# Moving two more units of a product to GpSimd, and shifting the offsets of GpSimd's operands, in a four-layer state-space kernel

## The chip, the core and the metric

The kernel runs on one core of one Trainium2 chip, in float32. The metric is the device time of one execution, in microseconds; before the change the median of three runs is 19150.31 us (19148.47 to 19160.53).

## What is computed

Eight images of 48 x 48 pixels and 96 channels pass through four layers, each with a group norm ahead of it and a residual sum behind it. Layers 0 and 3 (`ss2d`) and layer 2 (`lines`) are selective scans over the pixels in four directions, with 192 inner channels and 16 states; layer 1 (`spectral`) is a filtered two-layer network. The core of a scan layer is, for each direction:

```
def step(h, inp):
    u, dl, Bv, Cv = inp
    dA = jnp.exp(dl[..., None] * A)
    h = h * dA + (dl * u)[..., None] * Bv[:, :, None, :]
    y = jnp.einsum('bkdn,bkn->bkd', h, Cv)
    return (h, y)
...
delta = jax.nn.softplus(dts + dt_projs_bias)
_, ys = jax.lax.scan(step, h0, (u_t, d_t, B_t, C_t))
ys = jnp.moveaxis(ys, 0, -1) + xs * Ds
```

Here u is a convolved and Silu-gated input, dl (delta) a step size for each channel and pixel, and B and C are 16 numbers for each pixel. In ss2d one scan runs over all 2304 pixels of an image; in lines each of the 48 rows or columns starts from zero again.

## The kernel before

**Tiling.** A direction of an image is cut into five blocks of columns, four of 480 pixels and one of 384 (BLKS). With 8 images and 4 directions a scan layer has 160 blocks, and the three scan layers 480. The 192 channels x 16 states of a block are 24 *units* of 128 partitions (32 channels x 4 states) by n pixels. Three units make a *slot* (ORDER: channel half and group of four states), two slots a *turn*, four turns a block. Slots 0 and 1 belong to turn 0, up to 6 and 7 in turn 3.

**What a turn does.** All of it is in `scans`. A room (tile `dbu`, six units of m columns) is filled, scanned and multiplied in place:
- `make_dbu` (line 257) multiplies du by B. Even slots do their three units on VectorE. Odd slots are split by ON_POOL: so many of the last units on GpSimd, the others on VectorE. VectorE reads B from a copy in PSUM (`ps_b`, one bank), which `copy_b` (line 238) makes on ScalarE, seven times a block; GpSimd reads it from SBUF (`bc`).
- `make_da` (line 281) makes exp(dl x A) on ScalarE into `ps_da`, two units to a pair and two such tiles.
- `scan` (line 289) runs the recurrence on VectorE over a pair of units, three times a turn.
- `make_hc` (line 295) multiplies three units by C in place on GpSimd, twice a turn.
- `reduce` (lines 315 and 317) sums over states on TensorE.

**Order.** There is no scheduler: the program order in the turn loop is each engine's order. On VectorE a turn is: scan of pair 0, product of the next turn's even slot, scan of pair 1, product of the next turn's odd slot, scan of pair 2. So slots 2 and 3 are filled in turn 0, slots 4 and 5 in turn 1, 6 and 7 in turn 2, and the next block's 0 and 1 in turn 3. On GpSimd it is: product with C of the last turn's odd slot, product with B for the next turn's odd slot, product with C of this turn's even slot. `aside`, called twice a turn, puts in between: loads, one step of a neighbour image's convolution or norm (`side`), and a step of `stage1`, which prepares the block after the next. In ss2d, stage1's softplus (line 648, with a table load before it and one behind it) falls into turn 3 and du = dl x u (line 439, GpSimd) into the ends of turn 3 and turn 0. In lines, a Silu (line 808) falls into turn 1, one (line 766) into turn 3, a softplus (line 794) and du into turn 0. Also in lines, the gated result is projected (line 831, TensorE) and added to x (lines 837 and 839, VectorE) in turn 1.

**Layout.** Blocks of lines have m = n columns. In ss2d a unit has m = n + 2: a column that comes from the block before and one that goes to the next, one at each end, with the pixels between them (`at` starts at 1); blocks alternate in direction, so that a room's last column is the next block's first. delta and du lie side by side in `dds` (line 427 stores them to DRAM, line 212 loads them back repeated over partitions as `dd`). A `bc` tile holds one zero, then n values of B, then n of C, so that B with its leading zero starts at 0 and C at 1 + n.

The GpSimd products that the change shifts besides these are du (line 439) and the gate of the output (line 563, y times z).

Of the kernel before, what the change touches and what calls it, by code (L numbers as in the profile page):

```python
# [9 lines left out]
F32 = mybir.dt.float32  # L10
# [7 lines left out]
DH = 96  # L18
# [4 lines left out]
P = 128  # L23
SEG = 48
BLKS = [(0, 10), (10, 10), (20, 10), (30, 10), (40, 8)]
BMAX = 480
WMAX = BMAX + 2
NG = 8
ORDER = [(0, sg) for sg in range(4)] + [(1, sg) for sg in range(3, -1, -1)]
LOAD_BC = (2, 3, 6, 7)  # L30
# [1 line left out]
NBUF = 6  # L32
# [4 lines left out]
NM = 3  # L37
FAR = 1e30
CH = 96
ON_POOL = {1: 1, 3: 2, 5: 2, 7: 2}  # L40


DIRS_SS = [(False, False), (True, False), (False, True), (True, True)]
# [15 lines left out]
class Block:  # L59
# [9 lines left out]
    def columns(self, restart):  # L69

        self.mirrored = not restart and self.blk % 2 == 1
        self.back = self.rev != self.mirrored
        if restart:
            self.m = self.n
            self.at = self.by = slice(0, self.n)
            return
        self.m = self.n + 2
        self.at = slice(1, self.n + 1)
        self.came, self.goes = (self.m - 1, 0) if self.back else (0, self.m - 1)

        self.by = slice(0, self.n + 1) if self.back else slice(1, self.n + 2)

# [11 lines left out]
def vss_stack_kernel(ctx: ExitStack, tc: tile.TileContext, i: dict, out: bass.AP):  # L94
    nc = tc.nc
# [88 lines left out]
    def scans(dirs, order, restart, a, pools, ps, stage1, opening, done, side, tail):  # L184
# [6 lines left out]

        blocks = [Block(job, k, blk, n == 0, n == len(BLKS) - 1, dirs[k][1])
                  for job in range(nb) for k in order
                  for n, blk in enumerate(range(len(BLKS))[::-1 if dirs[k][1] else 1])]
# [2 lines left out]
        turns = [(b, q) for b in blocks for q in range(NG // 2)]  # L199
        nt = len(turns)  # L200
        rooms = [pools["dbu"].tile([P, 6 * WMAX], F32, tag="dbu", name="dbu") for _ in range(NG // 2)]
        bufs = [pools["bc"].tile([P, 1 + 2 * BMAX], F32, tag=f"bc{n}", name=f"bc{n}") for n in range(NBUF)]
        for buf in bufs:
            nc.gpsimd.memset(buf[:, 0:1], 0.0)
        dbus, das, bps, bcs, ys = {}, {}, {}, {}, {}
        later, ends = {}, []
        free = {n: 0 for n in range(NBUF)}
# [7 lines left out]
        def load_bc(t):  # L215

            b, slot = blocks[t // NG], t % NG
            sg = ORDER[slot][1]
            other = t - slot + NG - 1 - slot
            n = min(free, key=lambda n: free[n])  # L220
            free[n] = other
            r = bufs[n]
            rows4 = b.bcd[8 * sg:8 * sg + 8, :].rearrange("(s w) n -> s (w n)", w=2)
            nc.sync.dma_start(r[:, 1:1 + 2 * b.n], rows4.unsqueeze(0).to_broadcast([32, 4, 2 * b.n]))

            lead = b.at.start
            bcs[t] = bcs[other] = r[:, 1 - lead:1 - lead + b.m], r[:, 1 + b.n:1 + 2 * b.n]

        def copy_b(t):

            if t >= NG * len(blocks):
                return
            b, slot = blocks[t // NG], t % NG
            if slot == NG // 2:
                bps[t] = bps[t - 1]
                return
            bps[t] = ps("b", 1)
            nc.scalar.copy(bps[t][:, :b.m], bcs[t][0])  # L238

        def units(tile, b, lo, hi):  # L240
            return tile[:, lo * b.m:hi * b.m].rearrange("p (u m) -> p u m", m=b.m)
# [182 lines left out]
        b.bcd = pools["dr"].tile([2 * NS, b.n], F32, tag=f"bcd_{b.n}", name="bcd")  # L424

    def store_dd(b, half):
        nc.sync.dma_start(b.dd[half].rearrange("j (g m) -> g j m", g=3), b.dds[:, half, :2 * b.m])

    def sizes(b, half):

        t = b.dds[:, half]
        return [t[:, n * b.m:(n + 1) * b.m][:, b.at] for n in range(2)]

    def make_du(b, half, u):


        n = b.n
        dt, du = sizes(b, half)
        nc.gpsimd.tensor_mul(rows(du, n), rows(dt, n), u)  # L439
        if b.m == b.n:  # L440
            at = SEG - 1 if b.rev else 0
            nc.gpsimd.memset(rows(dt, n)[:, :, at:at + 1], FAR)
        elif half == 0:
            ends = b.dds[:, :, :2 * b.m].rearrange("p h (t m) -> p h t m", t=2)
            nc.gpsimd.memset(ends[:, :, :, b.came:b.came + 1], FAR)
            nc.gpsimd.memset(ends[:, :, :, b.goes:b.goes + 1], 0.0)


    def ss2d(l, xin, xout, b0=0):
        stack = ExitStack()  # L450
        pools, ps = scan_pools(stack)
# [3 lines left out]
        wt, big, zp, lnp, xio = pool("wt", 1), pool("big", 3), pool("z", 1), pool("ln", 2), pool("xio", 2)  # L455
# [21 lines left out]
        us, yss, zs = {}, {}, {}  # L477
# [38 lines left out]
        def post(b, blks=BLKS):  # L516

            y = yss[b]
            var = small.tile([CH, L // CH], F32, tag="var", name="var")
            v0, v1 = min(r0 for r0, nr in blks) * W // CH, max(r0 + nr for r0, nr in blks) * W // CH  # L520
            for r0, nr in blks:
                n = nr * SEG
                s = slice(r0 * W, r0 * W + n)
                pm = side_psum()
                for half in range(2):
                    nc.tensor.matmul(pm[:DH, :n], lhsT=mean, rhs=y[:, half, s], start=(half == 0), stop=(half == 1))
                yield
                yc = y[:, :, s]
                nc.vector.tensor_sub(yc, yc, pm[:DH, :n].unsqueeze(1).to_broadcast([DH, 2, n]))
                yield  # L530
                sq = lnp.tile([DH, 2, BMAX], F32, tag="sq", name="sq", bufs=1)
                nc.scalar.activation(sq[:, :, :n], yc, AF.Square)
                yield
                pv = side_psum()
                for c in range(n // CH):
                    for half in range(2):
                        nc.tensor.matmul(pv[:CH, c:c + 1], lhsT=sq[:, half, c * CH:(c + 1) * CH], rhs=ones,
                                         start=(half == 0), stop=(half == 1))
                yield
                nc.vector.tensor_copy(var[:, r0 * W // CH:(r0 * W + n) // CH], pv[:CH, :n // CH])  # L540
                yield
            nc.scalar.activation(var[:, v0:v1], var[:, v0:v1], AF.Sqrt, bias=eps5[:CH])
            yield
            nc.vector.reciprocal(var[:, v0:v1], var[:, v0:v1])
            yield
            for r0, nr in blks:
                n = nr * SEG
                s = slice(r0 * W, r0 * W + n)
                z = lnp.tile([DH, 2, BMAX], F32, tag="zin", name="zin", bufs=1)
                nc.sync.dma_start(z[:, :, :n], zs[b][:, :, s])  # L550
                xi = xio.tile([C, BMAX], F32, tag="xi", name="xi")
                nc.sync.dma_start(xi[:, :n], xin[b][:, s])
                pr = side_psum()
                for c in range(n // CH):
                    at = r0 * W // CH + c
                    nc.tensor.matmul(pr[:DH, c * CH:(c + 1) * CH], lhsT=var[:, at:at + 1].to_broadcast([CH, DH]),
                                     rhs=wc["ident"], start=True, stop=True)
                yield
                for half in range(2):
                    nc.vector.scalar_tensor_tensor(y[:, half, s], y[:, half, s], w[f"{l}_nw"][:, half:half + 1], pr[:DH, :n],  # L560
                                                   ALU.mult, ALU.mult)
                yield
                nc.gpsimd.tensor_mul(y[:, :, s], y[:, :, s], z[:, :, :n])
                po = side_psum()
                for half in range(2):
                    nc.tensor.matmul(po[:C, :n], lhsT=wnb[:, half, :], rhs=z[:, half, :n], start=(half == 0), stop=False)
                yield
                for half in range(2):
                    nc.tensor.matmul(po[:C, :n], lhsT=w[f"{l}_out"][:, half, :], rhs=y[:, half, s],
                                     start=False, stop=(half == 1))  # L570
                yield
                nc.vector.tensor_add(xi[:, :n], xi[:, :n], po[:C, :n])
                yield
                nc.sync.dma_start(xout[b][:, s], xi[:, :n])
# [38 lines left out]
        def stage1(b):  # L613
            n = b.n
            u = b.view(us[b.job], dirs[b.k][0])
# [23 lines left out]
                raw(0)  # L639

            def s4():
                b.dds = pools["dds"].tile([DH, 2, 2 * WMAX], F32, tag="dds", name="dds")
                biased(0)
                raw(1)

            def s6():
                both = b.dds[:, :, b.at]
                nc.scalar.activation(both, both, AF.Softplus)  # L648

            def du(half):  # L650
# [35 lines left out]
    def lines(xin, xout):  # L686
        stack = ExitStack()
        pools, ps = scan_pools(stack)
# [15 lines left out]
        for name in ("l2_outpt", "l2_out", "l2_inu"):  # L704
            shape = i[name].shape
            t = pools["dbu"].tile([P, 6 * WMAX], F32, tag="dbu", name="dbu")
            t = t[:shape[0], :int(np.prod(shape[1:]))]
# [35 lines left out]
        def stage1(b):  # L743
            n = b.n
# [44 lines left out]

            def s6():  # L790
                nc.sync.dma_start(b.bcd, b.bcl[:2 * NS, :n])
                b.dds = pools["dds"].tile([DH, 2, 2 * WMAX], F32, tag="dds", name="dds")
                for half in range(2):
                    nc.scalar.activation(sizes(b, half)[0], got[half][:DH, :n], AF.Softplus,  # L794
                                         bias=w["l2_dtb"][:, b.k, half:half + 1])
# [353 lines left out]
```

## Time and profile before

The profile is one execution: 19152.15 us, of which the span from the first to the last instruction is 19150.3 us.

| Stage | us from the start |
|---|---|
| ss2d, layer 0 (first scan 119, last 5827) | 119 to 5827 |
| spectral, layer 1 | 5827 to 7260 |
| lines, layer 2 | 7260 to 13276 |
| opening of layer 3 | 13276 to 13404 |
| ss2d, layer 3 | 13404 to 19118 |

| Group | count | busy us | mean ns |
|---|---|---|---|
| VectorE scan, line 289 | 5760 | 11863.3 | 2072 |
| GpSimd product with C, line 295 | 3840 | 10685.9 | 2796 |
| ScalarE exponential, line 281 | 11520 | 7428.3 | 648 |
| VectorE product with B, line 257 | 3840 | 4414.3 | 1150 |
| GpSimd product with B, line 257 | 1920 | 3101.7 | 1615 |
| ScalarE copy of B, line 238 | 3360 | 1805.0 | 537 |
| GpSimd du, line 439 | 640 | 815.1 | 1274 |

Means mix shapes: 480 and 384 columns, one to three units. A line of the timeline gives the start in us, the duration in us, the engine, the source line, the operation, what it writes and reads, and in brackets how long its engine was idle before it and what ended that. Instructions of one engine overlap a little in the records (a scan of 2.16 us is followed by the next instruction 2.07 us after its start), so a duration is not quite what an engine loses by an instruction; from start to start is. A line of the waits gives the total, how many times, and the longest.

### The profile page before, as it was taken

What the parts mean: (1) busy time and instruction counts of PE and PEld (TensorE: products, weight loads), DVE (VectorE), ACT (ScalarE), POOL (GpSimd) and SP (SyncE); (2) the same over time, 40 slices, a digit from 0 to 9 for tenths busy, and PEclk for the clock granted to TensorE, in tenths of its full rate; (3) what the DMA queues carried; (4) which work ended last, traced back from release to release, by engine and by line L of the source; (5) the groups of instructions that cost most, each with busy time, mean ns of one, the idle gap of its engine ahead of it and who ended that gap; (6) DMA issues with size and microseconds to landing.
All of it is one profiled execution on the core that took longest, in us unless ns stands there. A gap on an engine that the chain in (4) does not pass through costs nothing.

```text
span 19150.3 us, 170303 instructions
## 1 busy us (share of the span) xinstructions
PE 15031.5 (78%) x53500; PEld 4344.3 (23%) x53500; DVE 16643.8 (87%) x11289; ACT 14070.7 (73%) x20982; POOL 15110.6 (79%) x8304
## 2 busy tenths in 40 slices
PE   6777777777777997888888888887677777777776
PEld 1211211211214562222222222222121121121121
DVE  7999999999993227999999999997999999999998
ACT  6777877877872227888888888886778778778776
POOL 6899999899891006777777777776898998999998
PEclk7776776776767777887888888888777677677676
DMA  4444444444443324444444444443444444444444
GB/s 136 166 160 162 165 162 165 164 164 163 159 169 61 48 44 141 152 145 150 149 146 151 143 152 149 144 150 123 161 165 158 165 165 158 165 165 161 163 163 143
DMA packets 768469, 2831.72 MB, mean 148 GB/s; under 512 B 235724, under 2 KB 298668, under 8 KB 640926
## 3 DMA queue, kind: packets, MB, share of 16 engines
q1 hardware_dynamic: 767558, 2820.84, 44.7%
q8 instruction: 418, 6.85, 0.2%
q14 instruction: 493, 4.04, 0.1%
HBM read 2373.39 MB, written 447.18 MB: 147 GB/s over the span
## 4 chain that ended last, share of the span: by engine, by line
DVE 26%; PE 22%; ACT 18%; issue 16%; POOL 13%; DMA 4%; SPq 0%; DVEq 0%; POOLq 0%; ACTq 0%
DVE dbu L289 15%; POOL dbu L295 10%; DVE dbu L257 10%; PE ps_s L759 5%; ACT ps_da L281 5%; ACT L281 4%; PE ps_y L315 3%; PE ps_h L989 2%; POOL dbu L257 2%; PE ps_side L501 2%; PE ps_y L1002 2%; PE ps_s L831 1%; PE ps_s L630 1%; DMA dd<-dd 1%; DMA dd<-dds 1%
## 5 line engine op out<-in xcount | busy, mean ns | idle before, releaser
L289 DVE TENSOR_TENSOR_SCAN dbu<-ps_da,dbu 128x964 f32<-128x964 f32 (+3 forms) x5760 | 11863.3, 2072 | 884.6 <-ACT ps_da L281 862.4
L295 POOL TENSOR_TENSOR dbu<-dbu,bc 128x1440 f32<-128x1440 f32 (+1 forms) x3840 | 10685.9, 2796 | 2290.8 <-DVE dbu L289 2202.6
L281 ACT ACTIVATE ps_da<-dd,w_l_a 128x482 f32<-128x482 f32 (+3 forms) x11520 | 7428.3, 648 | 2851.4 <-DVE dbu L289 2636.8
L315 PE MATMUL ps_y<-dbu,w_red 128*32 128x480 f32 (+1 forms) x23040 | 4910.5, 745 | 2690.4 <-POOL dbu L295 2684.9
L317 PE MATMUL ps_y<-dbu,w_red 128*32 128x480 f32 (+1 forms) x7680 | 4869.1, 745 | 0.0
L257 DVE TENSOR_TENSOR dbu<-dd,ps_b 128x1443 f32<-128x1443 f32 (+10 forms) x3840 | 4414.3, 1150 | 264.6 <-ACT ps_b L238 217.0
L257 POOL TENSOR_TENSOR dbu<-dd,bc 128x962 f32<-128x962 f32 (+6 forms) x1920 | 3101.7, 1615 | 79.6 <-DMA dd<-dd 39.7
L315 PEld LDWEIGHTS ps_y<-dbu,w_red 128*32 128x32 f32 x23040 | 757.2, 126 | 6562.2 <-POOL dbu L295 4864.9
L238 ACT COPY ps_b<-bc 128x482 f32<-128x482 f32 (+3 forms) x3360 | 1805.0, 537 | 319.2 <-DVE dbu L257 288.5
L759 PE MATMUL ps_s<-xpad,w_l_cw 128*128 128x480 f32 (+1 forms) x2560 | 1758.4, 840 | 2.3 <-ACT xpad L142 1.6
L501 PE MATMUL ps_side<-xpad,w_l_cw 128*128 128x480 f32 (+1 forms) x2880 | 1604.8, 685 | 4.5 <-ACT xpad L142 4.5
L281 ACT ACT_TABLE_LOAD x986 | 1265.0, 1283 | 17.6
L131 POOL MEMSET w_l_cw<- 128x1760 f32 (+1 forms) x3 | 5.8, 1941 | 1340.3 <-DVE x L969 1334.9
L439 POOL TENSOR_TENSOR dds<-dds,u 96x480 f32<-96x480 f32 (+1 forms) x640 | 815.1, 1274 | 199.7 <-ACT dds L648 199.7
L630 PE MATMUL ps_s<-u,w_l_xp 96*38 96x480 f32 (+1 forms) x1280 | 932.7, 869 | 2.8 <-ACT dds L624 1.5
L620 PE MATMUL ps_s<-bcl,dtw 6*96 6x480 f32 (+1 forms) x1280 | 837.9, 742 | 108.1 <-ACT dds L624 99.8
L311 PE MATMUL ps_y<-ysum,w_ident 96*96 96x480 f32 (+1 forms) x960 | 753.2, 875 | 118.2 <-ACT ysum L671 118.1
L501 PEld LDWEIGHTS ps_side<-xpad,w_l_cw 128*128 128x128 f32 x2880 | 567.5, 222 | 1119.5 <-issue 907.5
L759 PEld LDWEIGHTS ps_s<-xpad,w_l_cw 128*128 128x128 f32 x2560 | 524.0, 210 | 1085.0 <-issue 999.6
L317 PEld LDWEIGHTS ps_y<-dbu,w_red 128*32 128x32 f32 x7680 | 697.3, 126 | 0.0
L776 PE MATMUL ps_s<-ub,w_l_xp 96*38 96x480 f32 (+1 forms) x640 | 382.7, 734 | 245.8 <-ACT ub L766 245.8
L800 PE MATMUL ps_s<-xpad,w_l_inz 96*96 96x480 f32 (+1 forms) x640 | 494.0, 904 | 97.6 <-ACT dds L794 80.9
(146 smaller groups left out, 11996.1 us busy)
## 6 DMA issues: line engine op xcount, KB each, us to landing
dd<-dd SPq DMA_DIRECT2D x512, 1446.0 KB
bc<-bcd SPq DMA_DIRECT2D x1536, 480.0 KB
dd<-dd SPq DMA_DIRECT2D x256, 1440.0 KB
dd<-dds SPq DMA_DIRECT2D x512, 361.5 KB
dd<-dd SPq DMA_DIRECT2D x128, 1158.0 KB
bc<-bcd SPq DMA_DIRECT2D x384, 384.0 KB
dd<-dds SPq DMA_DIRECT2D x256, 360.0 KB
dd<-dd SPq DMA_DIRECT2D x64, 1152.0 KB
```

The lines of the kernel that those rows point to most:

```text
L238: nc.scalar.copy(bps[t][:, :b.m], bcs[t][0])
L257: engine.tensor_mul(o, du, by.unsqueeze(1).to_broadcast([P, hi - lo, by.shape[1]]))
L281: nc.scalar.activation(da[:, at:at + b.m], b.got[half][:, u % 3, 0, :], AF.Exp, scale=a[:, b.k, ci:ci + 1])
L289: nc.vector.tensor_tensor_scan(db, da, db, 0.0, ALU.mult, ALU.add)
L295: nc.gpsimd.tensor_mul(h, h, bcs.pop(2 * t + sub)[1].unsqueeze(1).to_broadcast([P, 3, n]))
L315: nc.tensor.matmul(y[32 * g:32 * g + 32, :n], lhsT=wc["red"][:, :32], rhs=hc[:, g, b.at], start=False, stop=(slot == 3))
L317: nc.tensor.matmul(y[DH:, :n], lhsT=wc["red"][:, 32:], rhs=hc[:, 2, b.at], start=(slot == 0), stop=(slot == 3))
L439: nc.gpsimd.tensor_mul(rows(du, n), rows(dt, n), u)
L501: nc.tensor.matmul(pu[:, :n], lhsT=flat[:, at:at + P], rhs=xpad[:, r0 + dy:r0 + dy + nr, dx:dx + W], start=(tap == 0), stop=(tap == 8))
L620: nc.tensor.matmul(got["p"][:DH, :n], lhsT=dtw[2 * NS:, b.k, half, :], rhs=b.bcl[2 * NS:, :n], start=True, stop=True)
L630: nc.tensor.matmul(got["p"][:NBC, :n], lhsT=w[f"{l}_xp"][:, b.k, half, :], rhs=u[:, half], start=(half == 0), stop=(half == 1))
L759: nc.tensor.matmul(got["u", half][:, :n], lhsT=flat[:, at:at + P], rhs=shifted(off), start=(tap == 0), stop=(tap == 3))
```

## The change

- ON_POOL goes from {1: 1, 3: 2, 5: 2, 7: 2} to {1: 2, 3: 2, 5: 3, 7: 2}: nine units of 24 on GpSimd in place of seven. Slot 5 has none left on VectorE, and its copy of B to PSUM is left out. In the built program VectorE has 480 products fewer, ScalarE 480 copies fewer, GpSimd as many products as before, of which 960 are one unit larger.
- In ss2d a unit is n + 4 columns wide in place of n + 2 (the pixels start at 1 as before; the two added columns lie at the end). A scan covers 2m columns, so 968 for 964.
- A `bc` tile begins with two zeros (LEAD) in place of one. `dds` begins two elements into its tile, and so does z of the output's gate.
- The rooms are set to zero once a layer; the columns that carry FAR and zero in `dds` are written as runs of three and one.

```diff
-WMAX = BMAX + 2
+WMAX = BMAX + 4
+LEAD = 2
...
-ON_POOL = {1: 1, 3: 2, 5: 2, 7: 2}
+ON_POOL = {1: 2, 3: 2, 5: 3, 7: 2}
...
-        self.m = self.n + 2
+        self.m = self.n + 4
         self.at = slice(1, self.n + 1)
-        self.came, self.goes = (self.m - 1, 0) if self.back else (0, self.m - 1)
+        self.came, self.goes = (self.n + 1, 0) if self.back else (0, self.n + 1)
...
-        bufs = [pools["bc"].tile([P, 1 + 2 * BMAX], F32, tag=f"bc{n}", name=f"bc{n}") for n in range(NBUF)]
+        bufs = [pools["bc"].tile([P, LEAD + 2 * BMAX], F32, tag=f"bc{n}", name=f"bc{n}") for n in range(NBUF)]
         for buf in bufs:
-            nc.gpsimd.memset(buf[:, 0:1], 0.0)
+            nc.gpsimd.memset(buf[:, :LEAD], 0.0)
+        for room in rooms:
+            nc.gpsimd.memset(room, 0.0)
...
-            nc.sync.dma_start(r[:, 1:1 + 2 * b.n], rows4.unsqueeze(0).to_broadcast([32, 4, 2 * b.n]))
-
-            lead = b.at.start
-            bcs[t] = bcs[other] = r[:, 1 - lead:1 - lead + b.m], r[:, 1 + b.n:1 + 2 * b.n]
+            nc.sync.dma_start(r[:, LEAD:LEAD + 2 * b.n], rows4.unsqueeze(0).to_broadcast([32, 4, 2 * b.n]))
+
+            lo, hi = LEAD - b.at.start, LEAD + b.n
+            bcs[t] = bcs[other] = r[:, lo:hi + b.at.start], r[:, hi:hi + b.n]
...
+            if ON_POOL.get(slot) == 3:
+                return
             bps[t] = ps("b", 1)
-            nc.scalar.copy(bps[t][:, :b.m], bcs[t][0])
+            nc.scalar.copy(bps[t][:, :bcs[t][0].shape[1]], bcs[t][0])
...
+    def make_room(b, pools):
+        b.room = pools["dds"].tile([DH, LEAD + 4 * WMAX], F32, tag="dds", name="dds")
+        b.dds = b.room[:, LEAD:LEAD + 4 * b.m].rearrange("p (h t m) -> p h t m", h=2, t=2)
...
-            ends = b.dds[:, :, :2 * b.m].rearrange("p h (t m) -> p h t m", t=2)
-            nc.gpsimd.memset(ends[:, :, :, b.came:b.came + 1], FAR)
-            nc.gpsimd.memset(ends[:, :, :, b.goes:b.goes + 1], 0.0)
+            far = b.dds[:, :, :, b.came:] if b.back else b.room[:, :4 * b.m].rearrange("p (u m) -> p u m", m=b.m)[:, :, :LEAD + 1]
+            nc.gpsimd.memset(b.dds[:, :, :, 0:1] if b.back else b.dds[:, :, :, b.goes:], 0.0)
+            nc.gpsimd.memset(far, FAR)
...
-                z = lnp.tile([DH, 2, BMAX], F32, tag="zin", name="zin", bufs=1)
-                nc.sync.dma_start(z[:, :, :n], zs[b][:, :, s])
+                z = lnp.tile([DH, LEAD + 2 * BMAX], F32, tag="zin", name="zin", bufs=1)
+                z = z[:, LEAD:LEAD + 2 * n].rearrange("p (h n) -> p h n", h=2)
+                nc.sync.dma_start(z, zs[b][:, :, s])
```

More of the change, by code (lines that the diff above doesn't have):

```diff
@@ L426, in store_dd @@
     def store_dd(b, half):
-        nc.sync.dma_start(b.dd[half].rearrange("j (g m) -> g j m", g=3), b.dds[:, half, :2 * b.m])
+        nc.sync.dma_start(b.dd[half].rearrange("j (g m) -> g j m", g=3), b.dds[:, half].rearrange("p t m -> p (t m)"))
     def sizes(b, half):
-        t = b.dds[:, half]
-        return [t[:, n * b.m:(n + 1) * b.m][:, b.at] for n in range(2)]
+        return [b.dds[:, half, n, b.at] for n in range(2)]
+    def make_room(b, pools):
+        b.room = pools["dds"].tile([DH, LEAD + 4 * WMAX], F32, tag="dds", name="dds")
+        b.dds = b.room[:, LEAD:LEAD + 4 * b.m].rearrange("p (h t m) -> p h t m", h=2, t=2)
     def make_du(b, half, u):
@@ L562, in post @@
                 yield
-                nc.gpsimd.tensor_mul(y[:, :, s], y[:, :, s], z[:, :, :n])
+                nc.gpsimd.tensor_mul(y[:, :, s], y[:, :, s], z)
                 po = side_psum()
@@ L641, in s4 @@
             def s4():
-                b.dds = pools["dds"].tile([DH, 2, 2 * WMAX], F32, tag="dds", name="dds")
+                make_room(b, pools)
                 biased(0)
@@ L646, in s6 @@
             def s6():
-                both = b.dds[:, :, b.at]
+                both = b.dds[:, :, 0, b.at]
                 nc.scalar.activation(both, both, AF.Softplus)
@@ L791, in s6 @@
                 nc.sync.dma_start(b.bcd, b.bcl[:2 * NS, :n])
-                b.dds = pools["dds"].tile([DH, 2, 2 * WMAX], F32, tag="dds", name="dds")
+                make_room(b, pools)
                 for half in range(2):
```

## The prediction

> **What bounds the kernel now.** I read the page's busy line first, then the same by stage, then the waits, then single turns in the timeline. On the page VectorE leads.
>
> ```profile
> PE 15031.5 (78%) x53500; PEld 4344.3 (23%) x53500; DVE 16643.8 (87%) x11289; ACT 14070.7 (73%) x20982; POOL 15110.6 (79%) x8304
> ```
>
> The table by stage (first ss2d layer, then the lines layer; columns PE, PEld, DVE, ACT, POOL busy) shows that the share is an average over unlike stages.
>
> ```profile
> 119.00:5827.00 5708.00, 4279.91 (x15200) 1082.87 (x15200) 5381.31 (x3493) 4410.10 (x6647) 5157.93 (x2841) 0.71 0.48 162
> 7260.00:13276.00 6016.00, 5126.35 (x15952) 1340.47 (x15956) 5554.10 (x3766) 4886.27 (x7073) 4732.68 (x2552) 0.83 0.42 147
> ```
>
> In an ss2d layer VectorE is busy 94% of the time and GpSimd 90%; in the lines layer 92% and 79%. Who waits for whom in the first ss2d layer:
>
> ```profile
> POOL dbu L295 <- DVE dbu L289: 524.9, 511, 5.8
> DVE dbu L289 <- ACT ps_da L281: 277.4, 240, 3.8
> ACT bcl L635 <- PE ps_s L630: 206.3, 106, 5.8
> ```
>
> VectorE waits almost only for ScalarE's exponentials; its scans wait for GpSimd 3.4 us in the whole layer. So a faster GpSimd is worth little by itself. What counts is VectorE's work, but only in turns where ScalarE is not later. The end of a block in an ss2d layer is such a place (VectorE, then ScalarE):
>
> ```profile
> 2001.39 2.16 DVE L289 TENSOR_TENSOR_SCAN dbu<-ps_da,dbu 128x964 f32<-128x964 f32 x1
> 2003.47 1.13 DVE L257 TENSOR_TENSOR dbu<-dd,ps_b 128x962 f32<-128x962 f32 x1
> 2004.52 2.16 DVE L289 TENSOR_TENSOR_SCAN dbu<-ps_da,dbu 128x964 f32<-128x964 f32 x1
> 2007.11 2.17 DVE L289 TENSOR_TENSOR_SCAN dbu<-ps_da,dbu 128x964 f32<-128x964 f32 x1 [0.43 <-ACT ps_da L281]
> ```
>
> ```profile
> 2001.51 0.56 ACT L238 COPY ps_b<-bc 128x482 f32<-128x482 f32 x1 [0.18 <-DVE dbu L257]
> 2002.10 1.28 ACT L648 ACT_TABLE_LOAD   x1
> 2003.39 1.01 ACT L648 ACTIVATE dds<-dds 96x960 f32<-96x960 f32 x1
> 2004.42 1.28 ACT L281 ACT_TABLE_LOAD   x1
> 2005.71 1.36 ACT L281 ACTIVATE ps_da<-dd,w_l_a 128x482 f32<-128x482 f32 x2
> ```
>
> The ScalarE row from the copy to the two exponentials starts when VectorE has ended the product of slot 0, ahead of slot 1's product, and ends after VectorE is ready. Time taken from slot 1's product is lost here.
>
> **VectorE loses two units a block.** From start to start a unit costs VectorE 0.546 us, two 1.047 and three 1.549 (the trace's 481-column products that follow without a gap; busy means 0.63, 1.13, 1.63). Slot 1 goes from two units to one (0.50), slot 5 from one to none (0.55). In blocks of 384 columns it is 0.40 and 0.45. There are 480 blocks, 384 long and 96 short: 384 x 1.047 + 96 x 0.847 = 483 us if all of it counted. It doesn't, by turn:
> - Slot 1 stands in turn 3. I sorted the scans by place in the block: the first scan of turn 0 has no room after its exponentials in 129 of an ss2d layer's 160 blocks and in 159 of the lines layer's. The room in the others, at most 0.5 us each, sums to 14 us an ss2d layer and 0 in lines.
> - Slot 5 stands in turn 1. In ss2d the next turn's first scan comes 1.14 us (median) after its exponentials, twice what is taken away: all counts, 128 x 0.546 + 32 x 0.446 = 84 us a layer.
> - In lines, turn 1 holds ScalarE's Silu, and ScalarE decides in 84 of 160 blocks. There the removed copy counts:
>
> ```profile
> 9912.12 1.36 ACT L281 ACTIVATE ps_da<-dd,w_l_a 128x480 f32<-128x480 f32 x2 [0.94 <-DVE dbu L289]
> 9913.67 0.56 ACT L238 COPY ps_b<-bc 128x480 f32<-128x480 f32 x1 [0.18 <-DVE dbu L257]
> 9914.25 1.28 ACT L808 ACT_TABLE_LOAD   x1
> 9915.55 1.02 ACT L808 ACTIVATE zb<-ps_s 96x480 f32<-96x480 f32 x2
> 9916.59 1.28 ACT L281 ACT_TABLE_LOAD   x1
> 9917.88 1.36 ACT L281 ACTIVATE ps_da<-dd,w_l_a 128x480 f32<-128x480 f32 x2
> ```
>
> Slot 5 needs no copy in PSUM any more, so the table load at 9914.25 can start at 9913.50, when the exponentials end: 0.73 us earlier, with all behind it. 84 x 0.73 + 76 x 0.546 = 103 us, times 0.96 for the short blocks 99. VectorE's add of line 839 at the end of this turn waits for TensorE in 92 blocks; in the turn shown TensorE waits for the same Silu to free its bank, so I let it come earlier too. Against this stand the dd loads: they ended VectorE's wait in 29 blocks (39.8 us), and their chain now has up to 0.6 us less; I take 20 us off. Left: 79.
>
> **GpSimd gains two units and changes its offsets.** Product with C (three units of 480, in place), singly and by group in lines:
>
> ```profile
> 2003.63 3.07 POOL L295 TENSOR_TENSOR dbu<-dbu,bc 128x1440 f32<-128x1440 f32 x1 [1.36 <-DVE dbu L289]
> 2008.14 2.90 POOL L295 TENSOR_TENSOR dbu<-dbu,bc 128x1440 f32<-128x1440 f32 x1
> ```
>
> ```profile
> L295 POOL TENSOR_TENSOR dbu<-dbu,bc 128x1440 f32<-128x1440 f32 x1022 | 2784.3, 2734 | 956.8 <-DVE dbu L289 879.6 <-DMA bc<-bcd 77.1
> ```
>
> Take tiles to start on a 16-byte line, and count places in elements modulo 4. C lies at 1. In ss2d a unit is 482 wide, so the even slot's h lies at 1, 3, 1 (two units like C) and takes 3.07; the odd one's at 3, 1, 3 (one like C) takes 2.90. In lines h lies at 0 throughout and takes 2.73. So each unit aligned like C costs about 0.17 us. After the change h is at 1 and C at 2 in ss2d, 0 and 2 in lines. I take 2.73 for all, by the products with B, whose operands are one or two apart and which take 1.04 for one unit in either case. The other bound is 3.24 (three slow units), because a row speaks for it: line 439 takes 1.20 us for 480 contiguous elements in ss2d, at 1 against 0, no faster than in lines at 0 against 0. Which operand leads may matter; the change puts h behind C, as in the fast rows.
>
> A long ss2d block on GpSimd: 4 x 0.34 + 4 x 0.17 = 2.0 us less; two more units at 1.89 - 1.04 = 0.85 each, 1.7 more; about even. In lines only the 1.7 is added, against 1144 us of waiting for scans per layer. The Trainium skill weighs against both halves. "GPSIMD Engine Reference", Engine selection, sends elementwise work to VectorE, GpSimd being about 2x slower on two inputs: the rows say 0.85 against 0.55, so each move costs 0.3 us of engine time. By that rule the products stay; by the waits, VectorE's time is the dear one. "SBUF — State Buffer", Specifications, has 16-byte lines and a penalty for each crossing; any contiguous float stream crosses one in four elements whatever its start, so the rule gives the offsets nothing, and GpSimd +1.7 us a block (second rival). The 3.07 and 2.73 rows decide for me.
>
> What waits behind slot 5's product: in turn 1 GpSimd then has three pieces of 2.69 from start to start, 8.07 against VectorE's new 7.75, so the next products with C and TensorE's sums of them come some 0.3 us later in that turn. Its own reader is the second scan of turn 2, over 5 us off. Earlier products with C at a block's border help instead: TensorE's line 630 is queued behind their sums, ScalarE's copy at line 635 behind that, and 45 blocks an ss2d layer lose 56 us in turn 1's second scan so. Up to 0.45 us sooner in each gives 18 us a layer.
>
> **Small parts.** A scan over 968 instead of 964 elements: (2153 - 1753) / 192 = 2.08 ns an element, 8 ns each, 1920 scans a layer, four fifths on the path: -13 us an ss2d layer. Four memsets of 128x2904, some 2.5 us each from the 128x2500 row (2186 ns), run in each stage's opening, where GpSimd is idle (the first scan starts at 119 us): 0, at most 30 in all. More semaphore waits on GpSimd (353, at 43 ns each in the trace) lie in its idle time. DMA rows grow by 0.4%: 0, as the wait rows show ss2d's loads early. The FAR and zero memsets stay two a block, about 0.1 us each: 0.
>
> **Sum.** ss2d: 2 x (84 + 14 + 18 - 13) = 206. Lines: 79. Together 285 us off the profiled run's 19,152.15 us (span 19,150.3): 18,867. That run lies 1.8 us above the median of the three, so 18,865.
>
> **Rivals.**
> - *All of VectorE's saving counts*, if the ScalarE row in turn 3 shifts earlier too: 483 - 32 = 451 us, 18,700. Its anchor at slot 0's product speaks against it. 12%.
> - *The offsets do nothing*: GpSimd is 1.7 us a block fuller, TensorE's sums come later, and the 106 waits of line 635 grow instead of shrinking. Losing the 18 us and 40 more a layer: 285 - 116, 18,980. 20%.
> - *The new offsets are the slow kind for all three units* (slower): 3.24 us, 3.2 from start to start. A long ss2d block on GpSimd is then 8 x 3.2 + 8.2 (products with B) + 2.9 (line 439, memsets) = 36.7, and with 0.5 of waiting 37.2 against some 36.2 now: 1.0 x 320 x 0.96 = 307 more, less 79 in lines: 19,380. It decides from about 3.0 us a product. Line 439 speaks for it, every product with B against. 8%.
>
> The forecast has 60%; its own range is 18,790 to 18,960. From the cases: faster 0.89, same 0.03, slower 0.08, where "same" is within 0.2% of before, about what a measurement of this kernel can tell. The range runs from the first rival to beyond the second: 18,700 to 19,060.
>
> **What would show it.** The product with C at 2.73 in all layers (else rival two or three); VectorE's 128x962 products gone and 128x481 ones only in three of four turns; turn 1 at 7.75 us in ss2d and about 8.65 in lines, turn 3 of ss2d still at about 9.3; copies of line 238 down from 3360 to 2880. I am wrong if VectorE's scans start to wait for GpSimd, or if the wait for ps_da grows by more than slot 1's share.

## The result, and the profile after

The median went from 19155.42 us (four runs, 19148.47 to 19166.92) to 18846.06 us (four runs, 18839.27 to 18857.07): a ratio of 0.9838, interval 0.9821 to 0.9856, or 309 us less. The forecast was 18,865. The profiled execution took 18848.6 us, its span 18846.8.

The busy line of the page of the changed kernel:

```profile
PE 14864.5 (79%) x53500; PEld 4298.7 (23%) x53500; DVE 16139.5 (86%) x10809; ACT 13830.0 (73%) x20502; POOL 15203.6 (81%) x8316
```

VectorE lost 504 us and 480 instructions, which are the 480 pieces of slot 5; ScalarE lost 480 copies. Of VectorE's 504 us the span kept 303. The table by stage (first ss2d layer, then lines; columns as before) shows where:

```profile
119.00:5731.00 5612.00, 4190.40 (x15200) 1057.95 (x15200) 5219.81 (x3333) 4332.76 (x6487) 5088.34 (x2841) 0.73 0.49 165
7167.00:13075.00 5908.00, 5085.26 (x15952) 1325.51 (x15956) 5381.55 (x3607) 4800.52 (x6913) 4936.71 (x2552) 0.84 0.43 150
```

From first to last scan the two ss2d layers lost 96 and 104 us, lines 108; the rest of the span (openings, spectral layer, end) grew by 4. I then summed the lengths of the turns, from each turn's first scan to the next turn's, in us per layer:

| | turn 0 | turn 1 | turn 2 | turn 3 |
|---|---|---|---|---|
| first ss2d layer, before | 1484 | 1371 | 1350 | 1498 |
| first ss2d layer, after | 1481 | 1289 | 1342 | 1495 |
| lines, before | 1506 | 1532 | 1395 | 1578 |
| lines, after | 1505 | 1407 | 1396 | 1596 |

Nearly all of it is in turn 1, where slot 5 is filled. VectorE's timeline in the first ss2d layer after the change, from the last scans of a turn 3 to the next block's turn 2:

```profile
1971.49 0.63 DVE L264 TENSOR_TENSOR dbu<-dd,ps_b 128x481 f32<-128x481 f32 x1
1972.03 2.17 DVE L296 TENSOR_TENSOR_SCAN dbu<-ps_da,dbu 128x968 f32<-128x968 f32 x1
1975.12 2.17 DVE L296 TENSOR_TENSOR_SCAN dbu<-ps_da,dbu 128x968 f32<-128x968 f32 x1 [0.92 <-ACT ps_da L288]
...
1983.35 4.23 DVE L296 TENSOR_TENSOR_SCAN dbu<-ps_da,dbu 128x968 f32<-128x968 f32 x2
1987.49 1.63 DVE L264 TENSOR_TENSOR dbu<-dd,ps_b 128x1443 f32<-128x1443 f32 x1
1989.04 6.29 DVE L296 TENSOR_TENSOR_SCAN dbu<-ps_da,dbu 128x968 f32<-128x968 f32 x3
```

Two things are to be seen. At the block's border slot 1's product is one unit (0.63 us), and the wait of turn 0's first scan, 0.43 us at this kind of place before, is 0.92: the half microsecond became waiting. In turn 1 (from the second of the two scans at 1983.35) no product stands between the scans any more, and turn 2's first scan follows without a gap, as the third of the x3. The median turn 1 went from 8.30 to 7.76 us.

In lines, ScalarE's timeline in a turn 1:

```profile
9769.28 1.36 ACT L288 ACTIVATE ps_da<-dd,w_l_a 128x480 f32<-128x480 f32 x2 [0.94 <-DVE dbu L296]
9770.66 1.28 ACT L820 ACT_TABLE_LOAD   x1
9771.96 1.03 ACT L820 ACTIVATE zb<-ps_s 96x480 f32<-96x480 f32 x2
9773.00 1.28 ACT L288 ACT_TABLE_LOAD   x1
9774.29 1.36 ACT L288 ACTIVATE ps_da<-dd,w_l_a 128x480 f32<-128x480 f32 x2
```

The table load follows the exponentials at once; the copy between them is gone. The median turn 1 went from 9.35 to 8.64 us, against 8.65 forecast.

The waits in the first ss2d layer, after:

```profile
POOL dbu L302 <- DVE dbu L296: 461.2, 476, 5.8
DVE dbu L296 <- ACT ps_da L288: 315.8, 228, 4.1
ACT bcl L647 <- PE ps_s L642: 166.2, 66, 5.8
```

At turn 0's first scan VectorE waits 151 us in this layer, against 84 before: the saving of slot 1 went there. The row for exponentials shows only 38 us of it (315.8 against 277.4), because the view puts another 38 us of these waits down to GpSimd; in every one of them the exponentials ended no more than 0.11 us before the scan began, so that GpSimd was not what held it up. ScalarE's wait for line 642 fell by 40 us, and brought little, as shown below.

GpSimd's groups by form, whole execution (products with C, slot 5's products with B, du in ss2d and in lines):

```profile
L302 POOL TENSOR_TENSOR dbu<-dbu,bc 128x1440 f32<-128x1440 f32 x3072 | 8360.6, 2736 | 1560.2 <-DVE dbu L296 1412.0 <-DMA bc<-bcd 140.6 <-DMA dd<-dd 1.0
L264 POOL TENSOR_TENSOR dbu<-dd,bc 128x1443 f32<-128x1443 f32 x256 | 702.6, 2744 | 0.0
...
L449 POOL TENSOR_TENSOR dds<-dds,u 96x480 f32<-96x480 f32 x512 | 634.0, 1238 | 182.9 <-ACT dds L660 182.8
L449 POOL TENSOR_TENSOR dds<-dds,ub 96x480 f32<-96x480 f32 x256 | 264.6, 1033 | 13.9 <-ACT dds L806 13.9
```

The product with C takes 2736 ns in every layer, the 2.73 us that was taken. Three units with B take the same.

### The profile page after: what moved, and what is told of

Read it like the earlier page. It is cut to its first block, busy times and chain, and to the rows that moved or that the text cites. A ratio compares the mean times of both kernels' runs of the same rounds, so it can differ in the third digit from the quotient of the medians.

```text
span 18846.8 us, 169421 instructions
## 1 busy us (share of the span) xinstructions
PE 14864.5 (79%) x53500; PEld 4298.7 (23%) x53500; DVE 16139.5 (86%) x10809; ACT 13830.0 (73%) x20502; POOL 15203.6 (81%) x8316
## 4 chain that ended last, share of the span: by engine, by line
DVE 24%; PE 21%; ACT 18%; POOL 17%; issue 12%; DMA 7%; SPq 0%; POOLq 0%; DVEq 0%; ACTq 0%
DVE dbu L296 15%; POOL dbu L302 12%; DVE dbu L264 7%; ACT ps_da L288 5%; PE ps_s L771 4%; ACT L288 4%; POOL dbu L264 4%; DMA dd<-dd 3%; PE ps_y L322 3%; DMA dd<-dds 2%; PE ps_h L1001 2%; PE ps_y L1014 2%; POOL dds L449 1%; PE ps_side L512 1%; PE ps_s L642 1%
## 5 line engine op out<-in xcount | busy, mean ns | idle before, releaser
L296 DVE TENSOR_TENSOR_SCAN dbu<-ps_da,dbu 128x968 f32<-128x968 f32 (+3 forms) x5760 | 11853.6, 2076 | 1080.1 <-ACT ps_da L288 1002.8
L302 POOL TENSOR_TENSOR dbu<-dbu,bc 128x1440 f32<-128x1440 f32 (+1 forms) x3840 | 10060.1, 2634 | 1877.1 <-DVE dbu L296 1715.4
L288 ACT ACTIVATE ps_da<-dd,w_l_a 128x484 f32<-128x484 f32 (+3 forms) x11520 | 7440.1, 650 | 2865.8 <-DVE dbu L296 2652.9
L322 PE MATMUL ps_y<-dbu,w_red 128*32 128x480 f32 (+1 forms) x23040 | 4834.2, 736 | 2581.2 <-POOL dbu L302 2578.1
L324 PE MATMUL ps_y<-dbu,w_red 128*32 128x480 f32 (+1 forms) x7680 | 4795.5, 736 | 0.0
L264 DVE TENSOR_TENSOR dbu<-dd,ps_b 128x1443 f32<-128x1443 f32 (+7 forms) x3360 | 3895.9, 1159 | 292.9 <-ACT ps_b L245 217.5
L264 POOL TENSOR_TENSOR dbu<-dd,bc 128x962 f32<-128x962 f32 (+7 forms) x1920 | 3889.3, 2026 | 96.5 <-DMA dd<-dd 50.0
L245 ACT COPY ps_b<-bc 128x482 f32<-128x482 f32 (+3 forms) x2880 | 1543.4, 536 | 283.4 <-DVE dbu L264 257.3
L449 POOL TENSOR_TENSOR dds<-dds,u 96x480 f32<-96x480 f32 (+1 forms) x640 | 765.8, 1196 | 182.9 <-ACT dds L660 182.8
```

The costliest lines, as they stand in the source:

```text
L245: nc.scalar.copy(bps[t][:, :bcs[t][0].shape[1]], bcs[t][0])
L264: engine.tensor_mul(o, du, by.unsqueeze(1).to_broadcast([P, hi - lo, by.shape[1]]))
L288: nc.scalar.activation(da[:, at:at + b.m], b.got[half][:, u % 3, 0, :], AF.Exp, scale=a[:, b.k, ci:ci + 1])
L296: nc.vector.tensor_tensor_scan(db, da, db, 0.0, ALU.mult, ALU.add)
L302: nc.gpsimd.tensor_mul(h, h, bcs.pop(2 * t + sub)[1].unsqueeze(1).to_broadcast([P, 3, n]))
L322: nc.tensor.matmul(y[32 * g:32 * g + 32, :n], lhsT=wc["red"][:, :32], rhs=hc[:, g, b.at], start=False, stop=(slot == 3))
```

## The experiments

My theory: slot 5's unit pays in turn 1 of ss2d, the missing copy pays in turn 1 of lines, slot 1's unit pays next to nothing, and the offsets only make room on GpSimd. The rivals: the offsets bring the gain themselves; or slot 1 brings a good part of it; or the copy has no part in it.

**Offsets alone.** The changed kernel with the split of before:

```
-ON_POOL = {1: 2, 3: 2, 5: 3, 7: 2}
+ON_POOL = {1: 1, 3: 2, 5: 2, 7: 2}
```

> The new offsets with the old split (seven units on GpSimd). My theory: GpSimd was not what the turns waited for, so shorter products with C (2.73 us for 3.07 and 2.90) give only the earlier sums at a block's border, 2 x 18 us, less 2 x 13 us for the wider scans: about 19,140. Rival, that the offsets are what made the 309 us: about 18,850.

It measured 19108.84, ratio 0.9981 (0.9972 to 0.9989). That is 43 us by the medians, not 309: the rival that the offsets bring the gain falls. The ss2d layers lost 17 and 25 us, lines nothing. GpSimd's busy time in the first ss2d layer fell by 332 us (5158 to 4826), and the span took about a twentieth of that.

**Split alone.** The kernel before, with its old offsets and the new split:

```
-ON_POOL = {1: 1, 3: 2, 5: 2, 7: 2}
+ON_POOL = {1: 2, 3: 2, 5: 3, 7: 2}
...
+            if ON_POOL.get(slot) == 3:
+                return
```

> The new split (nine units, no copy for slot 5) on the old offsets: products with C stay at 3.07 and 2.90 us in ss2d. My theory: most of the gain stays, because slot 5's unit leaves VectorE all the same; lost are the earlier sums and some 40 us more a layer, gained back the wider scans: 18,846 + 2 x 45, about 18,935. Rival, that GpSimd has no room for two more units without the offsets: above 19,100, with scans waiting for GpSimd's products.

It measured 19032.61, ratio 0.9941 (0.9928 to 0.9955), between the two theories. Lines lost 107 us, all that the full change gives there; the ss2d layers lost only 9 and 14. Its first ss2d layer by stage, and VectorE's waits in it:

```profile
119.00:5818.00 5699.00, 4257.02 (x15203) 1075.78 (x15204) 5246.58 (x3333) 4326.42 (x6484) 5410.04 (x2840) 0.72 0.48 162
```

```profile
DVE dbu L291 <- ACT ps_da L283: 368.5, 252, 3.8
...
DVE dbu L291 <- POOL dbu L297: 5.5, 5, 1.2
```

GpSimd is busy 5410 of 5699 us, 95%, and yet VectorE's scans wait for it 5.5 us in all. GpSimd's lateness comes round by other ways. One is the exponentials: VectorE's wait for them is 53 us longer than in the changed kernel. The other one I had not thought of: four steps of the group norm on VectorE with 96 x 1 numbers each, part of the `side` work. Two of these steps in VectorE's groups by form in the first ss2d layer, in this kernel and then in the changed one:

```profile
L179 DVE SCALAR_TENSOR_TENSOR shift<-gm,rs 96x1 f32<-96x1 f32 x7 | 40.8, 5835 | 0.2
...
L167 DVE TENSOR_TENSOR dev<-mv,gm 96x1 f32<-96x1 f32 x7 | 15.5, 2218 | 0.2
```

```profile
L169 DVE TENSOR_TENSOR dev<-mv,gm 96x1 f32<-96x1 f32 x7 | 13.2, 1888 | 0.2
...
L181 DVE SCALAR_TENSOR_TENSOR shift<-gm,rs 96x1 f32<-96x1 f32 x7 | 3.3, 474 | 0.2
```

With the split alone, the step that writes `shift`, one number per partition with both operands in SBUF, takes VectorE 5.8 us in the mean. The reciprocal ahead of it, of the same size with one operand, takes 0.13. One such place in this kernel, VectorE's timeline and then GpSimd's:

```profile
1138.18 0.13 DVE L177 RECIPROCAL rs<-rs 96x1 f32<-96x1 f32 x1
1138.35 6.36 DVE L179 SCALAR_TENSOR_TENSOR shift<-gm,rs 96x1 f32<-96x1 f32 x1
```

```profile
1137.24 5.95 POOL L297 TENSOR_TENSOR dbu<-dbu,bc 128x1440 f32<-128x1440 f32 x2
1143.14 1.56 POOL L259 TENSOR_TENSOR dbu<-dd,bc 128x770 f32<-128x770 f32 x1
```

The step begins inside one product of GpSimd's and ends (1144.71) when the second product after that one has ended (1144.70), though it reads nothing that these products write. It is so throughout: in all eleven kernels that have these steps on VectorE, every step of 0.4 us or more (46 of the 128 before, 25 with the change, 46 with the split alone) ends 7 to 92 ns after the end of a GpSimd product. Summed over turn 2 of the first ss2d layer, these two-operand steps take 35.6 us before, 19.6 with the offsets alone, 60.3 with the split alone and 20.6 with both. That covers 25 of the 26 us by which turn 2 grows with the split alone. With the offsets alone the steps lose 16 us and turn 2 loses 11; of the other 5, some 4 are the wider scans (an estimate: 480 scans of 2161 ns in the mean in place of 2153). Split and offsets need each other in ss2d: the ratios of the two halves multiply to 0.992, and the whole is 0.984.

**Slot 1's unit back.**

```
-ON_POOL = {1: 2, 3: 2, 5: 3, 7: 2}
+ON_POOL = {1: 1, 3: 2, 5: 3, 7: 2}
```

> The changed kernel with slot 1 as before (one unit on GpSimd), so only slot 5's unit moved. My theory: slot 1's unit stands where ScalarE is later, so at most 2 x 14 us come back: 18,846 to 18,875. Rival, that each unit taken off VectorE counts alike (0.50 of 1.05 us a block): 309 x 0.48 = 148 us come back, 18,994.

It measured 18853.22, ratio 0.9846 (0.9832 to 0.9859): 7 us slower than the change by the medians, inside the intervals. In the first ss2d layer turn 3 is 13 us longer without the unit's move, and turns 0 and 1 are 4 and 9 us shorter; the layer is as long as with the change. So the unit's move does save what was forecast in its own turn (14 us), and the turns behind it give it back; why they do, no run here shows. Turn 0's first scan waits 88 us here and 151 with the unit moved. The rival, 18,994, falls.

**Slot 5's unit back.**

```
-ON_POOL = {1: 2, 3: 2, 5: 3, 7: 2}
+ON_POOL = {1: 2, 3: 2, 5: 2, 7: 2}
```

> The changed kernel with slot 5 as before (one unit on VectorE, with its copy on ScalarE), so only slot 1's unit moved. My theory: nearly all of the gain is lost, 2 x 84 us in ss2d and 100 in lines: about 19,115. Rival, that each unit counts alike: 161 us are lost, 19,007.

It measured 19094.6, ratio 0.9971 (0.9959 to 0.9982). Lines are back at 6015 us, turn 1 of the first ss2d layer at 1369. Slot 5 carries the change; the rival that shares it out (19,007) falls. The kernel with the offsets alone differs from this one by slot 1's unit only, and it is 14 us slower, with no overlap of the runs (19,105 to 19,124 against 19,088 to 19,098): with slot 5 left as before, the unit's move is worth a little.

**Slot 5 on GpSimd, but its copy kept.** ScalarE still copies B into PSUM for a slot that no longer reads it:

```
-            if ON_POOL.get(slot) == 3:
-                return
             bps[t] = ps("b", 1)
```

> The changed kernel, but slot 5's copy of B to PSUM is still made on ScalarE, read by nobody. My theory: in ss2d turn 1 is bound by VectorE and the copy costs nothing; in lines the Silu of turn 1 starts later again, 84 blocks x 0.73 us x 0.96 = 59 us: 18,905. Rival, that only VectorE's removed product counts: 18,846. Rival, that the copy decides everywhere: above 19,000.

It measured 18941.18, ratio 0.9895 (0.9879 to 0.9912). Its lines layer by stage:

```profile
7167.00:13172.00 6005.00, 5108.58 (x15948) 1336.54 (x15952) 5383.85 (x3606) 4886.60 (x7075) 4932.43 (x2552) 0.83 0.42 148
```

VectorE is as little busy as with the change (5384), and the layer is 97 us longer: 6005 against 6016 before. The theory had 59 us for the copy. Turn 1 is back at a median of 9.35 us, and VectorE's waits in it go from 87 us with the change to 192, of which those for TensorE's line 843 (841 here), whose sums VectorE adds to x, go from 63 to 144. So in lines, with the unit gone, the 0.56-us copy holds up 97 of the 108 us, and moving the unit without dropping the copy gives about 11. The opposite, the copy dropped and the unit kept, can't be had: VectorE's product reads the copy. The ss2d layers don't notice the copy (5612 in both).

**C aligned like h.** The `bc` tile keeps one leading element in place of two, so that C meets h, and B meets du, at equal places in ss2d, and C is one behind h in lines:

```
+BCLEAD = 1
...
-            lo, hi = LEAD - b.at.start, LEAD + b.n
+            lo, hi = BCLEAD - b.at.start, BCLEAD + b.n
```

> The changed kernel with one zero ahead of B in the bc tile, so that in ss2d all three units of h and C, and du and B, start at the same place modulo 16 bytes (in lines they stay one apart). My theory: a product with C takes 2.73 + 3 x 0.17 = 3.24 us in ss2d, a long block then has 37.7 us of GpSimd work against 35.7 now, and about 770 us come on top: 19,600. Rival, that GpSimd's durations don't bear on the time: 18,846.

**C one before h.** The same with `BCLEAD = 4`: C one element before h in ss2d, at the same place in lines.

> The changed kernel with four zeros ahead of B: in ss2d C then lies one element below h modulo 16 bytes in place of one above it, and B likewise against du; in lines both start alike. If only operands that start alike are slow: 2.73 us in ss2d, 3.24 in lines, about 19,030. If the order counts, as line 439 before the change suggests (1 against 0 was slow): 3.24 us in both, about 19,790.

They measured 19714.55, ratio 1.0296 (1.0281 to 1.0312), and 19841.07, ratio 1.0363 (1.0347 to 1.0378). GpSimd's groups by form in the first ss2d layer, of the first and then of the second kernel:

```profile
L303 POOL TENSOR_TENSOR dbu<-dbu,bc 128x1440 f32<-128x1440 f32 x1022 | 3301.0, 3248 | 87.8 <-DVE dbu L297 87.3
```

```profile
L303 POOL TENSOR_TENSOR dbu<-dbu,bc 128x1440 f32<-128x1440 f32 x1022 | 3296.6, 3244 | 92.8 <-DVE dbu L297 91.8
```

Both take 3.24 us, three slow units. In the second no operand is aligned like the other; what differs from the change is which one leads. The order of the operands counts. With 3.24 us GpSimd has 88 us of waiting left for scans in the layer, where the change leaves it 416, and it becomes the bound: the layer takes 6042 us. The norm's small steps grow with it: in turn 2 from 20.6 to 100.3 us, and that turn is 78 us longer than with the change.

**Slot 7's unit in place of slot 1's.** If slot 1's unit is worth nothing, its time on GpSimd is better spent in turn 2, which VectorE leads as it does turn 1:

```
-ON_POOL = {1: 2, 3: 2, 5: 3, 7: 2}
+ON_POOL = {1: 1, 3: 2, 5: 3, 7: 3}
```

> Nine units again, but the second moved unit is slot 7's and not slot 1's: slot 1 keeps two on VectorE, slots 5 and 7 have none there and no copy. My theory: slot 7 is filled in turn 2, which VectorE bounds in ss2d and in lines, so 0.55 us more a block count, while slot 1 gives back at most 7 us in all: about 18,620. Rival, that GpSimd is too full for it, or that the saving is lost to ScalarE as in turn 3: 18,850 or more.

It measured 18741.9, ratio 0.9788 (0.9774 to 0.9803): better than the change, and 122 us short of my number. Turn 2 lost 57 us in the first ss2d layer and 59 in lines; turn 3 gave 34 and 38 back. In the first ss2d layer 13 of the 34 are slot 1's own unit, which is on VectorE again, as the kernel with only that unit back shows; the other 21 are not explained. And the small norm steps of turn 2 went from 20.6 to 53.0 us.

**Those steps on ScalarE.** The changed kernel, with the norm's one-number steps on ScalarE (the copy `gm` goes along and takes a minus sign):

```
-        nc.vector.tensor_copy(gm, got["p"][:C, :1])
+        nc.scalar.activation(gm, got["p"][:C, :1], AF.Identity, scale=-1.0)
...
-        nc.vector.tensor_sub(dev, mv[:, 0:1], gm)
-        nc.vector.tensor_mul(dev, dev, dev)
-        nc.vector.tensor_add(dev, dev, mv[:, 1:2])
+        nc.scalar.activation(dev, gm, AF.Square, bias=mv[:, 0:1])
+        nc.scalar.activation(dev, dev, AF.Identity, bias=mv[:, 1:2])
...
-        nc.vector.scalar_tensor_tensor(shift, gm, -1.0, rs, ALU.mult, ALU.mult)
+        nc.scalar.activation(shift, gm, AF.Identity, scale=rs)
```

> The changed kernel with the four one-element steps of the norm's statistics (lines 167 to 171 and 181, 96x1) on ScalarE in place of VectorE. In the changed kernel those with two operands in SBUF take up to 2.6 us, 57 us in all beside the scans, the one-operand steps next to them 0.14. My theory: VectorE is held there while GpSimd reads SBUF, so some 50 us go: 18,795. Rival, that the time is a wait that only shows in these records and moves on with the work: 18,846.

It measured 18846.8, ratio 0.9842 (0.9829 to 0.9856): no gain. The step itself behaved. Its row in the view of the tile `shift` (shortest, median and longest ns):

```profile
L180 ACT ACTIVATE shift<-gm,rs x32: 275/294/296, 24.0 to 17721.8; 96x1 f32<-96x1 f32 x32
```

Turn 2 of the first ss2d layer lost 21 us, as much as the steps had taken, and the two layers 20 and 23. But lines grew by 11 us and the spectral layer by 20. There the steps now stand in ScalarE's order; that this is why is likely and not shown.

**Both.** Slot 7's kernel with the norm steps on ScalarE:

> Slot 7's unit on GpSimd in place of slot 1's, with the norm's small steps on ScalarE as well. In the run with slot 7 they took 119 us. My theory: that is what kept slot 7's saving at 104 us where 230 were forecast: 18,742 - 105, about 18,635. Rival, that GpSimd's fullness cost it elsewhere: within 30 us of 18,742.

It measured 18687.35, ratio 0.9761 (0.9748 to 0.9774). Turn 2 of the first ss2d layer went from 1285 to 1233 us: 52 of the 53 us that the steps had taken on VectorE came back.

**Slots 3, 5 and 7 wholly on GpSimd, slot 1 wholly on VectorE**, without and with the norm steps on ScalarE:

```
-ON_POOL = {1: 2, 3: 2, 5: 3, 7: 2}
+ON_POOL = {1: 0, 3: 3, 5: 3, 7: 3}
...
-            if slot == NG // 2:
+            if slot == NG // 2 and t - 1 in bps:
```

> Nine units as slots 3, 5 and 7 wholly on GpSimd and slot 1 wholly on VectorE; the copy of B for slot 3 goes too, slot 4 makes its own. Slot 1's two further units land in turn 3, where VectorE then has 9.33 us of work against a ScalarE row of the same length; slot 3's stands in turn 0. My theory: at most 84 us an ss2d layer and 80 in lines less than with slot 7 for slot 1, half of it by that run's measure: about 18,620. Rival, that turn 3 now grows by what turn 0 loses: 18,742.

> Slots 3, 5 and 7 on GpSimd, and the norm's small steps on ScalarE. If the two gains are separate: the run without the latter, less 50 to 110 us: about 18,540.

They measured 18695.47, ratio 0.9762 (0.9749 to 0.9775), and 18616.26, ratio 0.972 (0.9707 to 0.9734). The second beats both kernels and is the best version here: again nine of 24 units on GpSimd, but as three whole slots and none of slot 1. Its turns in the first ss2d layer are 1399, 1286, 1238 and 1571 us, and in lines 1404, 1456, 1345 and 1672: turns 0 to 2 are shorter than before in both, and turn 3, which has got slot 1 back whole, is 73 and 94 us longer. Both kernels took some 75 us more than I expected. In lines VectorE's waits for the dd loads in turn 3 went from 57 us with the change to 124 in the second, and turn 1 grew by 49 us (its waits for TensorE's line 843, 842 here, from 63 to 111); in the second, the spectral layer's 30 us come on top.

## Where the prediction was right and where not

Of the span, 285 us were forecast and 303 measured: 206 and 200 in the two ss2d layers, 79 and 108 in lines, and 4 lost in the rest. The total is closer than its terms are.

**Slot 5 in turn 1 of ss2d: right.** 84 us a layer forecast, 82 measured, and 7.75 us a turn forecast, 7.76 measured. The reason given held: VectorE alone was late there.

**Slot 5 in turn 1 of lines: right in mechanism, too small.** Forecast were 99 us from the turn, less 20 for the dd loads. The turn gave 125. The dd loads, in turn 3, then cost 18 (1578 to 1596; VectorE's wait for dd went from 39.8 to 57.4 us). The mis-sized term is "84 x 0.73 + 76 x 0.546": I counted the copy in 84 blocks only, and VectorE's unit in the other 76. The kernel with the copy kept shows that moving the unit with the copy left in gives 11 us; the copy counts in almost all blocks. 125 us over 160 blocks is 0.78 us each, 0.81 with the shorter blocks taken off: about 0.73, and somewhat more.

**Slot 1 in turn 3: worth less than the little forecast.** 14 us a layer in ss2d forecast; its own turn saves 13, and the neighbouring turns give it all back. The wait of turn 0's first scan went from 84 to 151 us in ss2d and from 174 to 238 in lines: the unit became waiting, as forecast. The sign of being wrong, that the wait for exponentials grows by more than slot 1's share, was not met: the share is 77 us a layer (128 x 0.50 + 32 x 0.40). Nor did the scans start to wait for GpSimd, as said above.

**Earlier sums at the block's border: failed.** The step "up to 0.45 us sooner in each gives 18 us a layer" took it that turn 1's second scan waits less when TensorE's sums come sooner. ScalarE's wait for line 642 did fall (206 to 166 us, 106 times to 66), and the gaps of that scan went from 56.2 to 53.2 us: 3 us, not 18. The copy at line 647 started sooner, and the exponentials behind it were set by something else, which no run here names.

**The norm's small steps: not foreseen, and nearly as large.** The faster products with C shortened VectorE's held steps by 15 us in the first ss2d layer and by 23 in the other, and turn 2, where they stand, by 8 and 15. So the sum of an ss2d layer (103 forecast, 96 and 104 measured) is right partly because wrong terms (18 and 14 for next to nothing) and a missing one are of a size. That part is luck.

**The second rival's mechanism was real, and too cheap.** With the old offsets, GpSimd was to cost 18 + 40 us a layer. The split alone loses 87 and 90 us a layer against the change; its forecast of 18,980 compares with 19,033. The price named TensorE's sums alone and had no held VectorE steps in it.

**The third rival's price was too cheap.** 19,380 had 307 us more for the two ss2d layers with slow products with C. In the kernel with C aligned like h they took 662 us more, and the whole 19,715. Two things were not in the price: the products with B were slow there too (2241 for 1891 ns for two units), and the norm's held steps grew by 65 and 57 us in turn 2 of the two layers. With C before h in ss2d, and level with it in lines, the time is 3.6% over that of before. The choice of 2.73 us rested on the rows whose second operand leads by one or two places, and line 439, left open, is explained by the order: its 1.20 us in ss2d had the second operand one place before the first.

**The two rules of the Trainium skill that the prediction weighed.** By the first ("GPSIMD Engine Reference", Engine selection), that VectorE is the faster engine for such products, the units would have stayed there. Each moved unit does cost GpSimd more than VectorE saves, and the time still fell, by 303 us of span for 504 us of VectorE's work. By the second ("SBUF — State Buffer", Specifications), of 16-byte lines, the offsets would have given nothing; the first ss2d layer's products with C went from 2990 to 2737 ns.

## What to carry to other kernels

Price a removed instruction in the turn where it stands, by the engine that is late there: a unit was worth 82 us a layer in one turn and next to nothing in another, and in lines the helper copy on ScalarE, once nobody read it, still held up nine times what moving the VectorE work had given. Follow a saved half microsecond to the next wait of the same engine before it is counted. And look at the smallest instructions of an engine that shares something with a loaded one: steps on one number per partition took 36 us of an ss2d layer's turn 2 before the change and 60 with the split alone, in groups too small to show on the page.

## What the runs showed of the hardware

**GpSimd's product of two operands depends on which one leads.** Let d be the start of the second operand less that of the first, in float32 elements modulo 4. All contiguous products fit: d = 1 or 2 is fast, d = 0 or 3 slow. Three units of 480 take 2.74 us with three fast ones, 2.90 and 3.07 with one and two slow ones, 3.24 with three; 0.17 us a unit. A product of du with 480 columns in lines went from 1.20 (d = 0) to 1.03 us (d = 2). In ss2d the mean of this product went only from 1.32 to 1.24 us: half the directions read u with a stride, and these still take 1.44. Why the order counts no run here shows.

**VectorE is held at small steps with two operands in SBUF while GpSimd works.** The step that writes `shift`, one number on 96 partitions, takes between 154 and 4305 ns in the kernel before, up to 2280 after, 6405 with the split alone and 9.2 us in the mean of the first ss2d layer with C aligned like h. Steps of the same size with one operand stay at 0.14 us, and the large scans and products, which read one operand from PSUM, keep means of 2.15 to 2.16 and 1.63 us in all the kernels. The Trainium skill has a mechanism for it ("SBUF — State Buffer", section "SBUF: two separate sides"): VectorE and GpSimd share a pair of ports as an exclusive lock, which a VectorE instruction with two inputs from SBUF and a GpSimd instruction that reads SBUF can't hold at once: the later one waits until the other has ended. The traces agree: of the norm's steps in question only those with two operands are held, and each held step ends with a GpSimd product. They differ from it in which product: the step of 6.36 us shown above began before two of the three that it waited for. It is not always so; at 225.96 us of the changed kernel a step of 2.62 us ends between two products that follow each other without a gap. What lets a step in between is open. That moving the steps away gives their time back in ss2d is shown.

**Left open.** Why turn 3 of ss2d grows by 21 us when slot 7's third unit goes to GpSimd, beyond the 13 of slot 1's unit, is not settled; its waits name several engines. Also open are what sets turn 1's second scan, since the earlier sums didn't, and why turns 0 and 1 give back what slot 1's unit saves in turn 3.
